# A macaron block with a long convolution: rows turned by VectorE instead of DMA transposes, and work moved between engines and steps

## The chip, the core and the metric

The kernel runs on one core of a Trainium2 chip. Its engines are TensorE (PE: matrix products; PEld is its weight load), VectorE (DVE), ScalarE (ACT), GpSimd (POOL) and SyncE (SP, which here only issues DMAs). Each engine works through its own instructions in order and waits for others by semaphores. The metric is the device time of one execution in microseconds (us).

## The reference

For x of 2 x 1024 rows of 1024 numbers, all float32:

```
x = x + 0.5 * ffn(layernorm(x))
x = x + s4(layernorm(x))
x = x + 0.5 * ffn(layernorm(x))

ffn(x): h = silu(x @ Wg) * (x @ Wu);  return h @ Wd     # 1024 -> 2752 -> 1024
        # weights of 4 bits, with scales and zero points by groups of 128 input rows
s4(x):  causal convolution of every row with a kernel of length 1024
        (made from the state space parameters), plus D[0] * x
```

Both feed-forward layers use the same weights.

## The kernel before

**Jobs.** The 2048 rows are four blocks of 512 (b = 0 to 3). A job is one feed-forward layer (k = 1 or 3) of one block; the eight jobs run in the order `JOBS = [(0,1), (1,1), (0,3), (1,3), (2,1), (3,1), (2,3), (3,3)]`, and the text calls them job 0 to job 7. Each job has an up stage (gate and up products) and a down stage. The convolution (k = 2) of a block runs inside the up stage of the job after its first layer: in jobs 1, 2, 5 and 6.

**Products.** Activations are split into two float16 parts, a high one and a low one (`hi`, `lo`), and each is multiplied by weights held as small whole numbers in bfloat16; so there are two products for each pair of weight chunk and input group. The scale of a group is applied by a rescale: the sum in PSUM is multiplied in place by the ratio of two groups' scales before the next group is added (`scaled`: by ScalarE on line 815, or by VectorE on line 819, as `on_act` says).

The up stage has 64 steps (`STEPS`): eight waves of three, later two, chunks of the inner dimension (`WAVES`), by eight input groups g. A step of three chunks has six units (gate and up of each chunk), 12 products of 512 columns (line 854) and a rescale of each unit; a step of two chunks has four units and eight products, in the last wave one unit more. Even units (gates) are rescaled by ScalarE, odd ones by VectorE, with the exceptions that the diff shows. After a wave's last group, `gated` makes silu(gate) on ScalarE (line 886), the product with the up part on VectorE (`hf`, line 889), and GpSimd makes the two float16 halves of h (`halves`, lines 894 and 895). `watch` puts two more GpSimd operations on a list of chores (lines 905 and 906), which are worked off one at a time.

The down stage has 44 steps, two halves of the output columns by 22 chunks. A step has four PSUM banks, eight products (line 962; the 22nd of each half has four) and four rescales, of which VectorE does two (c = 1 and 3), less those that `relief` names.

**The order of other work.** `hooks` hang work on a step number: `at(up, 36, f)` writes f's instructions ahead of the products of up step 36, and a half (36.5) in the middle of the step. The tile framework then plans the order on each engine by its own costs; `pinned` and `in_order_of_writing` bind instructions of the named engines to the order of writing. Weights are asked for on SP's queue (lines 788 and 795) six steps ahead, in job 0 four.

**Convolution.** For each of the four tiles t of 128 rows: VectorE normalizes and turns the rows in 32x32 blocks (lines 1669, 1673), SP stores them to DRAM (line 1677) and reads them back so that blocks stand in turned order (line 1684). GpSimd then makes sums of columns (lines 1345 to 1347), PE the products with the convolution's Toeplitz blocks in two parts (line 1351), and VectorE adds the results to x (lines 1381 to 1391). Job 1 starts this at step 36 with 3.5 steps between tiles, the others at step 23 with 4. Statistics for the third normalization (`moments_by_tile`, line 191, and `deviations_in_pieces`) follow in the same stage. Job 1's up stage also computes the convolution's kernel (`s4_tables`).

**Input of the next job.** In jobs 1 to 6 the next job's rows are normalized in place (`normalize`, line 274) and turned by `turn_by_dma`: four GpSimd operations make the float16 parts (lines 293 and 295), and two DMA transposes on SP's queue (lines 297 and 298) put them into `pieces`, which the next up stage reads as `xTh` and `xTl`. It hangs at steps 2 to 33 of the down stage. In job 0 the next job's input is turned by PE (`turn_by_pool`). The first job's own input is turned in eight chunks by PE (`first_turn`), ahead of its first steps.

**Results.** A down stage's result y is turned in 32x32 blocks by VectorE (line 1020), stored and read back, and added to x by GpSimd (line 1036).

Of the kernel before, what the change touches and what calls it, by code (L numbers as in the profile page):

```python
# [9 lines left out]
F32 = mybir.dt.float32  # L10
# [35 lines left out]
Q = 32  # L46
# [13 lines left out]
def macaron_s4_kernel(  # L60
# [38 lines left out]
    xpool = ctx.enter_context(tc.tile_pool(name="x", bufs=11))  # L99
    xtpool = ctx.enter_context(tc.tile_pool(name="xT", bufs=1))  # L100
    hpool = ctx.enter_context(tc.tile_pool(name="h", bufs=36))
# [174 lines left out]
    def turn_by_dma(b, t):  # L276

        k = ln[b, t][2]  # L280
        name = f"{b}_{k}_{t}"
        if b not in pieces:
            pieces[b] = [
                xtpool.tile([P, NC, TB], dt, tag=f"xT{w}", name=f"xT{w}_{b}_{k}")
                for w, dt in (("h", F16), ("l", F16))
            ]
        hi_t, lo_t = (a[:, :, bass.ts(t, P)] for a in pieces[b])
        halves = [slice(0, 512), slice(512, HID)]
        n = x[b][t]
        hi = hfpool.tile([P, HID], F16, tag="hf", name=f"hi_{name}")  # L290
        lo = gpool.tile([P, HID], F16, tag="g", name=f"lo_{name}")
        for own in halves:
            nc.gpsimd.tensor_copy(hi[:, own], n[:, own])
            yield
            nc.gpsimd.tensor_tensor(lo[:, own], n[:, own], hi[:, own], ALU.subtract)  # L295
            yield
        nc.sync.dma_start(hi_t, hi, transpose=True)
        nc.sync.dma_start(lo_t, lo, transpose=True)
# [522 lines left out]
    def gate_up(j, b, hooks):  # L821
        hi, lo = pieces[b]
        ps = {}
        for s, (wi, g) in enumerate(STEPS):
# [20 lines left out]
            for i, (k, pos, done) in enumerate(turns):  # L845
# [19 lines left out]
                if g < GK - 1:  # L865
                    on_act = unit % 2 == 0
                    if unit == 2 * fs[0 if n == 3 else 1] + 1:
                        on_act = (j == 0 and n == 3 and g in ((4, 6) if s < 8 else (0, 2, 4, 6)))
                        on_act = on_act or (j < 2 and g % 2 == 0 and (j or n == 2))
                        on_act = on_act or (j in (3, 4) and 24 < s < 33)  # L870
# [13 lines left out]
    def gated(j, f, pg, pu):  # L884
        g = gpool.tile([P, TB], F32, tag="g", name=f"g_{j}_{f}")
        nc.scalar.activation(g, pg, AF.Silu, scale=rat[:, 2 * f, GK - 1 :])  # L886
        hf = hfpool.tile([P, TB], F32, tag="hf", name=f"hf_{j}_{f}")
        last = rat[:, 2 * f + 1, GK - 1 :]
        nc.vector.scalar_tensor_tensor(hf, pu, last, g, ALU.mult, ALU.mult)  # L889
        two = t2(f"h_{j}_{f}").bitcast(F16).rearrange("p (i t) -> p i t", i=2)  # L890
        hi, lo = h[f] = two[:, 0], two[:, 1]

        def halves():
            nc.gpsimd.tensor_copy(hi, hf)  # L894
            nc.gpsimd.tensor_tensor(lo, hf, hi, ALU.subtract)  # L895

        halves()
        watch(hi)

    chores = []  # L900
# [39 lines left out]
    relief = {1: (2, 3, 6, 7, 14, 15, 20), len(JOBS) - 1: (36, 38, 40)}  # L940
# [67 lines left out]
    y_dram = [dpool.tile([TB, 512], F32, tag=f"yz{a}", name=f"yz{a}") for a in range(NH)]  # L1008
    s_dram = [dpool.tile([P, HID], F32, tag=f"sz{i}", name=f"sz{i}") for i in range(2)]
# [621 lines left out]
    def fast():  # L1631
# [5 lines left out]
        for j, (b, k) in enumerate(JOBS):  # L1637
# [7 lines left out]
            if prev:  # L1645
# [9 lines left out]
                if pk == 1:  # L1655
# [23 lines left out]
                    def columns_loaded(t):  # L1679
                        s4x[t] = s = t4(f"st_{pb}_{t}").rearrange("p (c t) -> p c t", c=NC)  # L1680
                        src = s_dram[t % 2].rearrange("(b i) (c a j) -> a i c b j", i=Q, a=NQ, j=Q)
                        for q in range(NQ):
                            dst = s[bass.ts(q, Q)].rearrange("p c (b j) -> p c b j", j=Q)
                            nc.sync.dma_start(dst, src[q])
# [10 lines left out]
                    for t in range(NT):  # L1695
# [6 lines left out]
                        at(up, o + (8 if ahead_of_split else 9), lambda t=t: conv(t))  # L1702
                        at(up, o + 10, lambda t=t: next(parts[t]))
                        at(up, o + 11, lambda t=t: next(parts[t], None))
                    steps = [(up, start_ + gap * t + 13 + i) for t in range(NT) for i in range(2)]
                    steps += [(up, start_ + gap * 3 + 14.5), (up, start_ + gap * 3 + 15)]
                    in_pieces(at, steps, lambda: moments_by_tile(pb, 3, True, LIFT))
                    done = start_ + gap * 3 + 15
                    steps = [(up, 62 + i / 2 if j == 1 else 51.5 + (3 * i // 2) / 2) for i in range(4)]
# [16 lines left out]
            if j == 0:  # L1726
# [25 lines left out]
                first_weights(up, dn, at)  # L1752
            if j == 1:
# [6 lines left out]
            if after:  # L1760
                ab, ak = after
                if ak == 1:
                    at(up, 55 if j == 0 else 6, pinned(lambda: load_x(ab, rows_of(u, ab)), ET.SP))
                    if j == 0:
                        steps = [(up, s) for s in (60.5, 61.5, 62.5)]
                        steps += [(dn, d) for d in (3, 4, 5, 10.5, 11.5, 12)]
                        in_pieces(at, steps, lambda: moments_by_tile(ab, 1, True, LIFT))
                        steps = [(dn, d) for d in (17.5, 18.5, 19, 19.5)]
# [8 lines left out]
                def turning(t):  # L1777
                    if t not in turns:
                        turns[t] = turn_by_dma(ab, t)
                    next(turns[t], None)  # L1780

                for t in range(NT):
                    for half in range(2):
                        d, where = (25 + 4 * t + 2 * half if j == 0 else (2, 6, 14, 20)[t] + half), dn
# [10 lines left out]
                    for d in (1, 3, 5, 7, 9):  # L1795
                        piece = lambda t=t: turning(t)
                        piece = lambda piece=piece: in_order_of_writing(piece, ET.Pool, ET.SP)
                        at(dn, 2 + 7 * t + d + (j == 1 and t == 0), piece)
# [87 lines left out]
    def first_turn(c):  # L1886
# [11 lines left out]
        if c not in (3, 5, 7):  # L1898
# [167 lines left out]
```

## Time and profile before

| | |
|---|---|
| median of 4 runs | 1970.77 us (1970.43 to 1971.83) |
| the profiled execution: its time, its span | 1971.39 us, 1969.3 us |
| granted clock of PE | 0.997 |
| busy: PE, DVE, ACT, POOL | 1927.4, 1627.7, 1403.8, 1044.2 us |
| rescales on ACT, up and down | 1284 x 660 ns, 669 x 662 ns |
| rescales on DVE, up and down | 1124 x 691 ns, 611 x 695 ns |
| 32x32 transposes on DVE (128x256) | 112 x 428 ns for y, 64 x 424 ns for the convolution |
| DMA transposes | 48 |

The span is the time from the first to the last instruction of the program in the profiled execution; what lies around it, here 2.1 us, is in the time of a run as well. Busy time counts an engine as busy while an instruction runs. Product records overlap, since products are pipelined: one of 512 columns has a record of some 379 ns, but in an undisturbed stage one starts every 0.216 us (543 in 117.21 us in job 3's up stage, by the chain).

### The profile page before, as it was taken

To read this page: it belongs to the slowest core of one execution; us is meant where nothing else is said; L and a number is where in the kernel's file an instruction comes from. 1 tells how busy PE (TensorE), PEld (TensorE's weight loads), DVE (VectorE), ACT (ScalarE), POOL (GpSimd) and SP (SyncE) were. 2 spreads that over 40 slices of the span, in tenths; PEclk is the share of its full clock that TensorE was granted. 3 is DMA by queue.
4 is the path that set the end of the run, shared out by engine and by line. 5 is a ranking of instruction groups with operands and counts; after the bars stand their busy time and mean duration, and the time that the engine had idled before them with its cause. 6 is when DMAs were issued, how large, how long until landed. Compare 5 with 4: busy or idle time off the path is not lost.

```text
span 1969.3 us, 28016 instructions
## 1 busy us (share of the span) xinstructions
PE 1927.4 (98%) x9202; PEld 926.8 (47%) x9202; DVE 1627.7 (83%) x2710; ACT 1403.8 (71%) x2205; POOL 1044.2 (53%) x1162
## 2 busy tenths in 40 slices
PE   6999999999999999999999999999999999999998
PEld 3444444464445544444444444456444564444443
DVE  7978878858888788877888778897888978887787
ACT  7888887738775577787777777764777646777776
POOL 5755668748465560656427660563614646345630
PEclk9999999999999999999999999999999999999999
DMA  6557553433635326622473236444264432563225
GB/s 213 194 183 227 175 150 95 119 97 105 202 112 138 94 81 199 211 67 76 128 252 120 69 86 192 134 115 113 77 183 149 124 102 76 153 204 99 73 71 176
DMA packets 320865, 267.34 MB, mean 136 GB/s; under 512 B 141773, under 2 KB 298518, under 8 KB 320710
## 3 DMA queue, kind: packets, MB, share of 16 engines
q1 hardware_dynamic: 319326, 262.87, 45.1%
q10 hardware_dynamic: 1160, 1.90, 0.3%
q8 instruction: 74, 1.21, 0.3%
q0 software_dynamic: 224, 0.69, 0.2%
q14 instruction: 81, 0.66, 0.1%
HBM read 195.58 MB, written 57.02 MB: 128 GB/s over the span
## 4 chain that ended last, share of the span: by engine, by line
PE 83%; DVE 9%; issue 3%; POOL 2%; ACT 1%; DMA 1%; SPq 0%; DVEq 0%; POOLq 0%; ACTq 0%
PE pg L854 50%; PE po L962 29%; DVE pg L819 4%; PE pc L1351 3%; PE pb L1351 1%; DVE hf L889 1%; DVE stats L191 1%; POOL h L895 1%; DVE x L274 0%; DVE xn L1669 0%; POOL h L894 0%; ACT pg L815 0%; DMA w<-wq 0%; ACT g L886 0%; POOL squared L905 0%
## 5 line engine op out<-in xcount | busy, mean ns | idle before, releaser
L815 ACT ACTIVATE pg<-pg,rat 128x512 f32<-128x512 f32 x1284 | 808.4, 660 | 379.5 <-PE pg L854 376.2
L854 PEld LDWEIGHTS <-w 128*128 128x128 bf16 x5504 | 538.1, 98 | 672.3 <-issue 42.7
L819 DVE TENSOR_TENSOR pg<-pg,rat 128x512 f32<-128x512 f32 x1124 | 743.1, 691 | 118.6 <-PE pg L854 114.0
L854 PE MATMUL pg<-xTl,w 128*128 128x512 f16 x2752 | 705.2, 379 | 9.3 <-DVE pg L819 6.8
L854 PE MATMUL pg<-xTh,w 128*128 128x512 f16 x2752 | 701.2, 380 | 3.6 <-ACT pg L815 1.0
L962 PE MATMUL po<-h,wd 128*128 128x512 f16 x2680 | 585.7, 379 | 1.7 <-DVE po L819 1.3
L815 ACT ACTIVATE po<-po,ratd 128x512 f32<-128x512 f32 x669 | 436.7, 662 | 116.3 <-PE po L962 113.8
L819 DVE TENSOR_TENSOR po<-po,ratd 128x512 f32<-128x512 f32 x611 | 422.5, 695 | 83.3 <-PE po L962 81.4
L962 PEld LDWEIGHTS <-wd 128*128 128x128 bf16 x2740 | 267.7, 98 | 325.9 <-issue 9.2
L894 POOL CAST h<-hf 128x512 f16<-128x512 f32 x168 | 106.4, 635 | 353.0 <-DVE hf L889 352.9
L906 POOL TENSOR_TENSOR most<-most,squared 128x512 f32<-128x512 f32 (+1 forms) x176 | 223.9, 1272 | 9.6
L1036 POOL TENSOR_TENSOR x<-x,yr 128x512 f32<-128x512 f32 x52 | 65.7, 1265 | 274.9 <-DMA yr<-yz 274.8
L895 POOL TENSOR_TENSOR h<-hf,h 128x512 f16<-128x512 f32 x168 | 195.5, 1167 | 10.6
L905 POOL TENSOR_TENSOR squared<-h 128x512 f32<-128x512 f16 x168 | 175.6, 1045 | 6.0
L889 DVE SCALAR_TENSOR_TENSOR hf<-pg,rat,g 128x512 f32<-128x512 f32 x168 | 121.0, 746 | 36.7 <-ACT g L886 28.3
L886 ACT ACTIVATE g<-pg,rat 128x512 f32<-128x512 f32 x168 | 110.1, 686 | 21.2 <-PE pg L854 11.7
L191 DVE BATCH_NORM_STATS2 stats<-x 128x6 f32<-128x512 f32 x88 | 59.6, 680 | 0.1
L295 POOL TENSOR_TENSOR lo<-x,hi 128x512 f16<-128x512 f32 x48 | 55.7, 1160 | 2.8
L1381 DVE TENSOR_TENSOR x<-x,pc 128x512 f32<-128x512 f32 x32 | 22.0, 688 | 34.5 <-PE pc L1351 34.5
L1351 PE MATMUL pc<-near,st 128*128 128x256 f32 (+1 forms) x256 | 48.6, 334 | 0.0
L1020 DVE STREAM_TRANSPOSE y<-y 128x256 f32<-128x256 f32 x112 | 47.9, 428 | 0.0
L1351 PEld LDWEIGHTS pc<-near,st 128*128 128x128 f32 x256 | 43.4, 195 | 7.3 <-issue 1.1
(225 smaller groups left out, 830.4 us busy)
## 6 DMA issues: line engine op xcount, KB each, us to landing
w<-wq SPq DMA_DIRECT2D x319, 192.0 KB
wd<-wdq SPq DMA_DIRECT2D x336, 128.0 KB
w<-wq SPq DMA_DIRECT2D x128, 128.0 KB
x<-in_L_attn_u_dram SPq DMA_DIRECT2D x30, 512.0 KB
yz<-y SPq DMA_DIRECT2D x56, 256.0 KB
yr<-yz SPq DMA_DIRECT2D x56, 256.0 KB
w<-wq SPq DMA_DIRECT2D x64, 160.0 KB
sz<-xn SPq DMA_DIRECT2D x16, 512.0 KB
```

Of the source, the lines that this page charges most:

```text
L191: nc.vector.bn_stats(stats[:, t, i, :], x[b][t][:, bass.ts(i, 512)])
L815: nc.scalar.activation(dst, src, AF.Copy, scale=sc)
L819: nc.vector.tensor_tensor(dst, src, sc.to_broadcast(list(dst.shape)), ALU.mult)
L854: product = lambda: nc.tensor.matmul(p, weights, (lo, hi)[k][:, g, :], start=(g == 0 and not done), stop=(g == GK - 1 and done), skip_grou ...
L886: nc.scalar.activation(g, pg, AF.Silu, scale=rat[:, 2 * f, GK - 1 :])
L889: nc.vector.scalar_tensor_tensor(hf, pu, last, g, ALU.mult, ALU.mult)
L894: nc.gpsimd.tensor_copy(hi, hf)
L895: nc.gpsimd.tensor_tensor(lo, hf, hi, ALU.subtract)
L905: chores.append(lambda: nc.gpsimd.tensor_tensor(own, hi, hi, ALU.mult))
L906: chores.append(lambda: nc.gpsimd.tensor_tensor(total, total, own, ALU.add))
L962: nc.tensor.matmul(ps[c], w[:, bass.ts(c, P)], part, start=(f == 0 and k == 0), stop=(f == NF - 1), skip_group_check=True,)
L1351: nc.tensor.matmul(dst, lhsT, rhs, start=start, stop=stop, skip_group_check=True)
```

## The change

- `turn_by_dma` goes. In jobs 1 to 6 the normalized rows are turned in place in 32x32 blocks by VectorE (`turn_blocks`, four operations a tile), stored to DRAM (`store_blocks`) and read back in turned order by four loads (`load_blocks`), and GpSimd splits them into the float16 parts (`split_columns`). Their steps: where the next job has k = 1 (jobs 3 and 4) the turn is in the up stage, elsewhere in the down stage.
- Rescales of one odd unit go to ScalarE in even groups of jobs 2, 5 and 6 too; some more in jobs 3 and 4; `relief` names more down steps in job 1 and new ones in jobs 2, 5 and 6.
- In job 1 the halves of chunks 15 to 18 are put off to steps 50.5, 51.5, 58 and 59; the convolution's sums and products come one step later in job 1, and in each job's last tile; the moments after them half a step later in job 1.
- In job 0 the rows for job 1 are loaded at step 46 instead of 55, their moments are taken in the up stage and the deviations earlier in the down stage. Chunks 4 and 6 of the first input are split by GpSimd instead of ScalarE and VectorE.
- One buffer more for tiles of x, one fewer for h.

```diff
-    xpool = ctx.enter_context(tc.tile_pool(name="x", bufs=11))
+    xpool = ctx.enter_context(tc.tile_pool(name="x", bufs=12))
-    hpool = ctx.enter_context(tc.tile_pool(name="h", bufs=36))
+    hpool = ctx.enter_context(tc.tile_pool(name="h", bufs=35))
...
-    def turn_by_dma(b, t):
...
+    def turn_blocks(b, t, i):
+        own = x[b][t][:, bass.ts(i, 256)]
+        nc.vector.transpose(own, own)
+    def store_blocks(b, t):
+        nc.sync.dma_start(t_dram[t], x[b][t])
+    def load_columns(dst, dram):
+        src = dram.rearrange("(b i) (c a j) -> a i c b j", i=Q, a=NQ, j=Q)
+        for q in range(NQ):
+            part = dst[bass.ts(q, Q)].rearrange("p c (b j) -> p c b j", j=Q)
+            nc.sync.dma_start(part, src[q])
+    def load_blocks(b, t):
+        tile_ = t4(f"turned_{b}_{ln[b, t][2]}_{t}").rearrange("p (c t) -> p c t", c=NC)
+        columns_of[t] = tile_
+        load_columns(tile_, t_dram[t])
+    def split_columns(b, t):
...
+        hi, lo = (a[:, :, bass.ts(t, P)] for a in pieces[b])
+        both = columns_of.pop(t)
+        for half in range(2):
+            own = slice(4 * half, 4 * half + 4)
+            nc.gpsimd.tensor_copy(hi[:, own], both[:, own])
+            yield
+            nc.gpsimd.tensor_tensor(lo[:, own], both[:, own], hi[:, own], ALU.subtract)
+            yield
...
                     if unit == 2 * fs[0 if n == 3 else 1] + 1:
                         on_act = (j == 0 and n == 3 and g in ((4, 6) if s < 8 else (0, 2, 4, 6)))
-                        on_act = on_act or (j < 2 and g % 2 == 0 and (j or n == 2))
-                        on_act = on_act or (j in (3, 4) and 24 < s < 33)
+                        on_act = on_act or (j in (0, 1, 2, 5, 6) and g % 2 == 0 and (j or n == 2))
+                        on_act = on_act or (j in (3, 4) and 24 < s < 40 and (s < 33 or g % 2 == 0))
...
-        halves()
+        if j == 1 and f in WAVES[5] + WAVES[6]:
+            put_off.append(halves)
+        else:
+            halves()
...
-    relief = {1: (2, 3, 6, 7, 14, 15, 20), len(JOBS) - 1: (36, 38, 40)}
+    relief = {1: range(2, 24, 2), len(JOBS) - 1: (36, 38, 40)}
+    for j in (2, 5, 6):
+        relief[j] = range(2, 20, 2)
...
-                        at(up, o + (8 if ahead_of_split else 9), lambda t=t: conv(t))
-                        at(up, o + 10, lambda t=t: next(parts[t]))
-                        at(up, o + 11, lambda t=t: next(parts[t], None))
-                    steps = [(up, start_ + gap * t + 13 + i) for t in range(NT) for i in range(2)]
-                    steps += [(up, start_ + gap * 3 + 14.5), (up, start_ + gap * 3 + 15)]
+                        late = j == 1 or t == NT - 1
+                        at(up, o + (8 if ahead_of_split else 9 + late), lambda t=t: conv(t))
+                        at(up, o + 10 + late, lambda t=t: next(parts[t]))
+                        at(up, o + 11 + late, lambda t=t: next(parts[t], None))
+                    ends = [start_ + gap * t + 13 + (j == 1) / 2 for t in range(NT)]
+                    steps = [(up, e + i) for e in ends for i in range(2)]
+                    steps += [(up, ends[-1] + 1.5), (up, ends[-1] + 2)]
...
+            for d in (50.5, 51.5, 58, 59) if j == 1 else ():
+                at(up, d, lambda: put_off.pop(0)())
...
-                    at(up, 55 if j == 0 else 6, pinned(lambda: load_x(ab, rows_of(u, ab)), ET.SP))
+                    at(up, 46 if j == 0 else 6, pinned(lambda: load_x(ab, rows_of(u, ab)), ET.SP))
                     if j == 0:
-                        steps = [(up, s) for s in (60.5, 61.5, 62.5)]
-                        steps += [(dn, d) for d in (3, 4, 5, 10.5, 11.5, 12)]
+                        steps = [(up, s) for s in (53, 53.5, 54, 54.5, 55, 55.5, 60, 60.5, 61)]
                         in_pieces(at, steps, lambda: moments_by_tile(ab, 1, True, LIFT))
-                        steps = [(dn, d) for d in (17.5, 18.5, 19, 19.5)]
+                        steps = [(dn, d) for d in (3.5, 4, 4.5, 5)]
...
-                        d, where = (25 + 4 * t + 2 * half if j == 0 else (2, 6, 14, 20)[t] + half), dn
+                        d, where = (25 + 4 * t + 2 * half if j == 0 else 2 + 4 * t + half), dn
...
-                    for d in (1, 3, 5, 7, 9):
-                        piece = lambda t=t: turning(t)
-                        piece = lambda piece=piece: in_order_of_writing(piece, ET.Pool, ET.SP)
-                        at(dn, 2 + 7 * t + d + (j == 1 and t == 0), piece)
+                    where, turn, kept, read, part = (
+                        (up, 33 + 2 * t, 35 + 2 * t, 39 + 2 * t, 2 + 3 * t)
+                        if ak == 1
+                        else (dn, 4 + 4 * t, 6 + 4 * t, 9 + 4 * t, 13 + 4 * t)
+                        if j == 1
+                        else (dn, 1 + 4 * t, 3 + 4 * t, 6 + 4 * t, 10 + 4 * t)
+                    )
+                    for i in range(4):
+                        at(where, turn + i / 2, pinned(lambda t=t, i=i: turn_blocks(ab, t, i), ET.DVE))
+                    at(where, kept, pinned(lambda t=t: store_blocks(ab, t), ET.SP))
+                    at(where, read, pinned(lambda t=t: load_blocks(ab, t), ET.SP))
+                    for i in range(4):
+                        at(dn, part + (3 * i // 2) / 2, pinned(lambda t=t: turning(t), ET.Pool))
...
-        if c not in (3, 5, 7):
+        if c < 3:
             nc.scalar.copy(hi, ps)
             nc.vector.tensor_tensor(lo, ps, hi, ALU.subtract)
         else:
```

## The prediction

> **What bounds the kernel now.** I read the page's chain of work that ended last, then busy time by stage, then the chain and the waits of TensorE (PE) inside the stages that stand out.
>
> ```profile
> PE 83%; DVE 9%; issue 3%; POOL 2%; ACT 1%; DMA 1%; SPq 0%; DVEq 0%; POOLq 0%; ACTq 0%
> PE pg L854 50%; PE po L962 29%; DVE pg L819 4%; PE pc L1351 3%; PE pb L1351 1%; DVE hf L889 1%; DVE stats L191 1%; POOL h L895 1%; DVE x L274 0%; DVE xn L1669 0%; POOL h L894 0%; ACT pg L815 0%; DMA w<-wq 0%; ACT g L886 0%; POOL squared L905 0%
> ```
>
> The products are the bound; no edit removes a product, so only time in which PE stands can be won. Busy time by stage (columns: stretch, its length, then busy us and instructions of PE, PEld, DVE, ACT, POOL, then clock, DMA share, GB/s) shows where it stands:
>
> ```profile
> 263.50:453.00 189.50, 182.47 (x905) 96.28 (x904) 147.38 (x277) 128.58 (x209) 127.97 (x170) 0.99 0.40 112
> 527.80:707.20 179.40, 176.54 (x882) 91.58 (x881) 154.89 (x266) 110.62 (x174) 97.72 (x100) 1.00 0.40 115
> 707.20:781.60 74.40, 74.40 (x346) 33.66 (x345) 60.83 (x94) 55.33 (x85) 25.74 (x28) 1.00 0.54 152
> 781.60:930.30 148.70, 148.64 (x689) 67.31 (x688) 122.44 (x198) 114.00 (x181) 87.93 (x87) 1.00 0.39 124
> ```
>
> These are job 1's up stage, job 2's up and down, and job 3's up. Job 3 has no convolution: 688 products in 148.7 us is the floor of an up stage, and 74.4 the floor of a down stage. Jobs 5 and 6 repeat job 2 (179.3, 179.4). What a convolution must cost is read from the last tile of job 1, in the chain in order of time; the same view shows what the first one waits for:
>
> ```profile
> 388.87 1.15 POOL h L895
> 390.02 0.55 POOL h L894
> ...
> 391.83 1.00 POOL sums L1345
> ...
> 435.97 1.75 PE pc L1351 x12
> 437.72 0.22 PE pb L1351 x2
> 437.95 2.65 PE pc L1351 x20
> 440.60 1.56 PE pb L1351 x14
> ```
>
> 6.18 us a tile, 24.7 for four. So job 2's up stage stands 179.4 - 148.7 - 24.7 = 6.0 us, jobs 5 and 6 the same: 18. Job 1's stands 189.5 - 148.7 - 24.7 = 16.1, less at most 4.8 us of products for the tables (L1194 1.8, L1304 2.0, L1277 1.0): 11.3. PE's own waits, first 360 to 455 us, then 615 to 710:
>
> ```profile
> PE pb L1351 <- POOL sums L1345: 5.4, 2, 3.6
> PE pg L854 <- ACT g L886: 0.6, 1, 0.6
> ```
> ```profile
> PE pg L854 <- DVE pg L819: 1.8, 5, 0.7
> PE pb L1351 <- POOL sums L1345: 0.4, 1, 0.4
> PE pg L854 <- ACT pg L815: 0.2, 1, 0.2
> ```
>
> The reader is to see two illnesses: in job 1 the sums stand behind two halves (L894, L895) in POOL's queue, and in jobs 2, 5, 6 rescales come late from a full VectorE (154.9 us in a stage whose products outside the convolution take 148.7). The list holds 2.4 of the 6.0; the rest lies in product records stretched by short waits. All that can be won is about 18 + 11 + a few in job 0.
>
> **The change, part by part.**
>
> *Rescales to ScalarE.* In the up stages of jobs 2, 5, 6 one more unit goes to ACT in the four even groups of each of eight waves: 32 a job, 22 us (0.69 each) off DVE, 21 us (0.66) onto ACT. DVE falls from 155 to 133 of 179, ACT rises from 111 to 132. Waits that DVE ended should mostly go. They come after each convolution (several adds and a rescale pile up) and at the stage's end, when x is normalized (L274). Next in line is ACT in the two-chunk waves: a step is 8 products, 1.73 us, and ACT then has three rescales in even steps, two in odd, and two gates: 18 x 0.66 + 2 x 0.69 = 13.3 of 13.8 us a wave. Queued back to back they pitch shorter, as job 0's timeline shows, five in 3.04:
>
> ```profile
> 156.40 3.04 ACT L815 ACTIVATE pg<-pg,rat 128x512 f32<-128x512 f32 x5 [0.29 <-PE pg L854]
> ```
>
> so 0.61 each, 12.4 of 13.8. Job 1 already runs this split with a convolution; there about 0.26 us is lost when ACT restarts after a tile, and 2.39 us of ACT lie on the chain in its last wave. I leave 2.3 of the 6.0 us: gain 3.7 a job (between 2.0, what the listed DVE and ACT waits hold, and 5.5), 11 for three. In jobs 3 and 4 three more rescales go over; no wait there to win.
>
> *Sums first, later products (job 1, and each last tile).* Four halves are put off to steps 50.5, 51.5, 58, 59, past the sums; products move one step later. A half pair is 0.61 + 1.15 us, two of them 3.5 us: the 3.6 us wait. Gain: the 5.4 us listed, and some of the restarts behind them: 7 (4 to 9). Price: the moments end half a step later, so the deviations lie nearer the stage's end; 0.5 us. The late halves cost nothing themselves: their products come at down steps 15 to 18, over 30 us later; and x rows have 12 buffers for 11, h 35 for 36, with no wait on either pool in the lists, so 0. In jobs 2, 5, 6 the 0.4 us wait is in the 3.7.
>
> *Rows turned by VectorE.* Per tile, 2 DMA transposes (1.25 us of SP's time each) become 4 DVE transposes, one store and four loads; the POOL work is the same four operations. 24 tiles: 96 x 0.43 = 41 us on DVE. Jobs 3 and 4 have them in the up stage, two a step at 33 to 40.5, where DVE (0.82 busy) has room: 0 (to 0.4 each). In the down stages of jobs 2, 5, 6, 4 x 0.43 = 1.7 us per four steps meets two rescales given to ACT, 1.4: even, but the first pair falls on steps 1 and 1.5, before any relief and while DVE still clears the last chunks: +0.3 each (0 to 0.7). In job 1's down stage x is normalized in the same steps, every two steps then hold 3 x 0.69 + 1.7 = 3.8 of 3.46 us by mean durations, though queued ones overlap by 0.1 each: +0.3 (0 to 1.5). These 1.2 us are paid; the transfer is not, as long as the prefetch covers it. It reads as the convolution's does, and the page by stretch shows one such read-back and one pair of DMA transposes:
>
> ```profile
> 605.00:610.00 5.00, 5.00 (x25) 2.25 (x23) 4.63 (x9) 3.62 (x7) 2.08 (x3) 1.00 0.89 236
> 726.00:731.00 5.00, 5.00 (x25) 2.27 (x24) 4.02 (x7) 3.88 (x6) 4.76 (x7) 1.00 0.95 179
> ```
>
> Both fill the engines, PE does not stand. The packet records say why they are equal: 4096 packets of 128 bytes at 12.9 ns are 3.31 us of sixteen engines, 2048 packets of 256 bytes at 27.8 ns are 3.56; the store adds 1.27. [...] The rows above are of this very read-back, whose runs are 32 elements since VectorE has already turned the blocks, so I take them.
>
> *Job 0.* Two of the first turns go from DVE (2 x 0.69 off) to POOL (2 x 1.77 on), at 31 and 38 us, where the chain runs through POOL (L685 four times, 3.13, then L410 to L412). Cost 0.5, between -1 (DVE was late there by 0.5 at 43.9) and +2.5 (all of one turn ahead of the scales, and more). Moments move from six places in the down stage to the up stage: 5 statistics of 0.68 leave a down stage that stands about 3 us, and come into steps 53 to 55.5, where DVE idles 1.9 us before the gates. -0.5 (-2 to +2). The rows of x for it, 2 MB, are loaded at step 46 instead of 55, ahead of weight loads on SP, some 10 us at that stage's 210 GB/s; it was as long at 55, and no wait for weights shows there: 0 (to 1). Job 0 together 0.
>
> **Sum.** -11 - 7 + 0.5 + 0.9 + 0.3 + 0 = -16.3, say -16.5. The profiled execution had 1969.3 us of span and 2.1 around it, 1971.4, which is 0.6 over the median of 1970.8. So the span goes to about 1952.8, the median to 1954.3.
>
> **Rivals.**
>
> *Only the POOL waits go (0.17).* ACT takes DVE's place in the narrow waves: 13.3 of 13.8 us leaves nothing for restarts, and job 1's last wave already ends on ACT. Then jobs 2, 5, 6 gain about 1 each: -3 - 7 + 1.7 + 0.5 = -8, 1963. Against it, the 0.61 pitch.
>
> *Nothing net (0.08).* The order on the engines is a planner's; with other lengths it can put the sums behind the halves again, or the late products against the next wave's banks. Then no step does what it says: 1967 to 1974.
>
> *SP's queue, slower (0.10).* Place: the 24 read-backs. SP works in order; a load that waits for its store to land holds the weight loads behind it. In 600 to 700 us SP already stood this long for one store:
>
> ```profile
> SPq L1714 <- DVE x L1391: 7.0, 1, 7.0
> ```
>
> Weights are asked for six steps ahead, 6 x 1.73 = 10.4 us in a down stage, and take about 3 us to come: it decides from about 7.4 us of standing. To eat the gain it needs 9 us at 16 tiles: 16 x 1.6 = 26 us, so 1980. Against it: the convolution's store and load, two steps apart, cause no wait for weights (1.3 us in all of the kernel's listed waits on w), and here three or four steps lie between.
>
> The other 0.65 is the forecast, by itself 1946 to 1961.
>
> **Numbers.** A measurement here can tell about 0.2%, 4 us, from no change. Faster: the forecast 0.65 and the first rival 0.15 of its 0.17: 0.80. Same: 0.09, from the second rival and the end of the first. Slower: 0.11, SP's queue and a bad start of job 0. The range runs from 1945 (nearly all 29 us but the price of the turns) to 1967, where the slower rival and some of the second are left out.
>
> **What would show it.** Up stages of jobs 2, 5, 6 at 175 to 176 us, DVE near 133 busy in them and ACT near 132; job 1's up near 183 with no wait on sums over 1 us; down stages under 75; no DMA_TRANSPOSE; 96 more of DVE's transposes; some 133 rescales fewer on L819 (96 and 6 up, 4 and 27 down). Wrong if PE waits for w, if up stages of jobs 2, 5, 6 keep over 178 us with ACT as releaser, or if job 0 grows by over 3 us.

## The result, and the profile after

The change does not make the kernel faster: 1972.4 us (median of 40 runs) against 1969.6 us (median of 60 runs of the kernel before beside them), ratio 1.0013 with a 95% interval of 1.0009 to 1.0018, so it is 2.8 us slower. The forecast was 1954.3. The profiled execution has a span of 1969.9 us, before 1969.3. The chain of work that ended last, by engine and by line:

```profile
PE 85%; DVE 7%; POOL 4%; issue 3%; ACT 1%; DMA 0%; ACTq 0%; POOLq 0%; DVEq 0%
PE pg L871 51%; PE po L984 29%; PE pc L1374 3%; DVE pg L836 2%; PE pb L1374 1%; POOL h L912 1%; DVE hf L906 1%; DVE po L836 1%; DVE x L274 1%; POOL most L926 1%; POOL h L911 1%; POOL squared L925 0%; DVE xn L1692 0%; ACT g L903 0%; ACT pg L832 0%
```

DVE's rescales of the up stages on the chain (pg L836, before pg L819) fell from 4% to 2%, as meant; POOL rose from 2% to 4%: its halves (L911, L912) and its chores (L925, L926). Busy time by stage of the kernel after, with the columns of the prediction's table. The rows are job 0 from its third step, job 1 up and down, job 2 up and down, job 3 up:

```profile
26.80:264.00 237.20, 232.35 (x1100) 107.27 (x1099) 196.66 (x325) 195.67 (x320) 153.71 (x199) 1.00 0.61 194
264.00:454.50 190.50, 183.44 (x905) 97.70 (x904) 148.21 (x276) 128.96 (x209) 128.15 (x170) 0.98 0.40 112
454.50:530.90 76.40, 75.12 (x345) 33.63 (x344) 64.38 (x110) 60.02 (x95) 55.90 (x54) 1.00 0.63 176
530.90:709.00 178.10, 175.97 (x881) 91.55 (x880) 136.24 (x234) 126.62 (x206) 97.82 (x100) 1.00 0.41 116
709.00:783.70 74.70, 74.65 (x346) 33.69 (x345) 59.25 (x101) 59.20 (x94) 26.03 (x28) 1.00 0.66 180
783.70:932.80 149.10, 148.87 (x689) 67.26 (x688) 124.94 (x211) 115.34 (x184) 87.97 (x87) 1.00 0.51 152
```

Two stages of before that the prediction did not show, the same part of job 0 and job 1's down stage:

```profile
28.50:263.50 235.00, 231.22 (x1101) 107.42 (x1100) 196.67 (x325) 196.28 (x320) 149.02 (x195) 1.00 0.61 194
453.00:527.80 74.80, 74.56 (x345) 33.64 (x344) 62.52 (x97) 57.90 (x91) 56.01 (x54) 1.00 0.53 152
```

Stage by stage, measured to 0.01 us from a stage's first product to the next stage's first:

| stage | before | after | difference |
|---|---|---|---|
| start, to job 0's third step | 28.48 | 26.77 | -1.71 |
| rest of job 0 | 234.98 | 237.27 | +2.29 |
| job 1 up | 189.55 | 190.48 | +0.93 |
| job 1 down | 74.80 | 76.41 | +1.61 |
| jobs 2, 5, 6 up, each | 179.38 | 178.07 | 3 x -1.31 |
| jobs 2, 5, 6 down, each | 74.40 | 74.65 | 3 x +0.25 |
| jobs 3, 4 up, each | 148.72 | 149.17 | 2 x +0.45 |
| jobs 3, 4 down, job 7 up | | | 0 |
| job 7 down, to the end | 85.02 | 84.80 | -0.22 |

The start is chance: in the profile of before the granted clock is 0.50 from 24.58 to 27.99 us, so that job 0's second step takes 4.29 us and not 2.60. The same half clock appears in three experiments that have the changed job 0, and in no other profile. Job 7's down stage, which no edit touches, takes 84.5 to 86.7 us in the twelve profiles. Without these two rows the sum is +2.6 us, and the medians differ by 2.8. PE's waits in the changed kernel, in three stretches: 360 to 456 us, job 2's up stage, job 1's down stage:

```profile
PE pb L1374 <- POOL sums L1368: 6.1, 2, 3.1
```
```profile
PE pg L871 <- DVE pg L836: 1.0, 2, 0.8
PE pb L1374 <- POOL sums L1368: 0.5, 1, 0.5
PE pg L871 <- ACT pg L832: 0.2, 1, 0.2
```
```profile
PE po L984 <- DVE po L836: 1.2, 3, 0.6
```

The wait for the sums that was to go is still there, 6.1 us where it was 5.4. The waits that VectorE ends in job 2 are nearly halved. Job 1's down stage has three, 1.2 us in all, where it had one of 0.2.

### The profile page after: what moved, and what is told of

Read it like the earlier page. It is cut to its first block, busy times and chain, and to the rows that moved or that the text cites. A ratio compares the mean times of both kernels' runs of the same rounds, so it can differ in the third digit from the quotient of the medians.

```text
span 1969.9 us, 28221 instructions
## 1 busy us (share of the span) xinstructions
PE 1928.7 (98%) x9202; PEld 928.0 (47%) x9202; DVE 1573.9 (80%) x2671; ACT 1467.9 (75%) x2338; POOL 1050.1 (53%) x1166
## 4 chain that ended last, share of the span: by engine, by line
PE 85%; DVE 7%; POOL 4%; issue 3%; ACT 1%; DMA 0%; ACTq 0%; POOLq 0%; DVEq 0%
PE pg L871 51%; PE po L984 29%; PE pc L1374 3%; DVE pg L836 2%; PE pb L1374 1%; POOL h L912 1%; DVE hf L906 1%; DVE po L836 1%; DVE x L274 1%; POOL most L926 1%; POOL h L911 1%; POOL squared L925 0%; DVE xn L1692 0%; ACT g L903 0%; ACT pg L832 0%
## 5 line engine op out<-in xcount | busy, mean ns | idle before, releaser
L832 ACT ACTIVATE pg<-pg,rat 128x512 f32<-128x512 f32 x1386 | 860.5, 661 | 333.7 <-PE pg L871 329.1
L836 DVE TENSOR_TENSOR pg<-pg,rat 128x512 f32<-128x512 f32 x1022 | 677.3, 692 | 153.9 <-PE pg L871 149.2
L832 ACT ACTIVATE po<-po,ratd 128x512 f32<-128x512 f32 x700 | 449.6, 662 | 105.0 <-PE po L984 102.4
L836 DVE TENSOR_TENSOR po<-po,ratd 128x512 f32<-128x512 f32 x580 | 399.8, 694 | 90.0 <-PE po L984 88.4
L911 POOL CAST h<-hf 128x512 f16<-128x512 f32 x168 | 106.4, 635 | 349.7 <-DVE hf L906 347.2
L926 POOL TENSOR_TENSOR most<-most,squared 128x512 f32<-128x512 f32 (+1 forms) x176 | 224.3, 1274 | 10.0
L912 POOL TENSOR_TENSOR h<-hf,h 128x512 f16<-128x512 f32 x168 | 195.5, 1167 | 10.8
L925 POOL TENSOR_TENSOR squared<-h 128x512 f32<-128x512 f16 x168 | 176.1, 1048 | 6.5
L314 POOL TENSOR_TENSOR xTl<-turned,xTh 128x512 f16<-128x512 f32 x48 | 55.4, 1155 | 3.4
L312 POOL CAST xTh<-turned 128x512 f16<-128x512 f32 x48 | 29.3, 610 | 42.1 <-DMA turned<-tz 39.9
L1368 POOL TENSOR_TENSOR sums<-st 128x384 f32<-128x384 f32 x16 | 16.1, 1008 | 58.6 <-PE pb L1374 48.0
```

What stands on the lines that cost most here:

```text
L832: nc.scalar.activation(dst, src, AF.Copy, scale=sc)
L836: nc.vector.tensor_tensor(dst, src, sc.to_broadcast(list(dst.shape)), ALU.mult)
L925: chores.append(lambda: nc.gpsimd.tensor_tensor(own, hi, hi, ALU.mult))
L926: chores.append(lambda: nc.gpsimd.tensor_tensor(total, total, own, ALU.add))
```

## The experiments

Each kernel is the changed kernel with the edit shown, unless it says otherwise; ratios are to the kernel before, run on the same chip.

**Are the late halves late?** In the changed kernel POOL's queue around the first and the third tile of job 1's convolution reads so (start, us, instruction):

```profile
391.05 0.61 POOL L911 CAST h<-hf 128x512 f16<-128x512 f32 x1
391.74 1.15 POOL L912 TENSOR_TENSOR h<-hf,h 128x512 f16<-128x512 f32 x1
392.85 1.17 POOL L1368 TENSOR_TENSOR sums<-st 128x384 f32<-128x384 f32 x1
...
419.28 0.61 POOL L911 CAST h<-hf 128x512 f16<-128x512 f32 x1 [13.46 <-DVE hf L906]
...
422.87 0.99 POOL L1368 TENSOR_TENSOR sums<-st 128x384 f32<-128x384 f32 x1
```

The halves still stand ahead of the sums. At 419.28 POOL had idled 13.46 us for a product of VectorE, with sums queued behind it whose data had been read back by 407.2 us. The first experiment binds the halves to the place where they are written:

```diff
-                at(up, d, lambda: put_off.pop(0)())
+                at(up, d, pinned(lambda: put_off.pop(0)(), ET.Pool))
```

> The changed kernel with one line more: the halves that are put off in job 1 are bound to GpSimd's order of writing, so behind the sums. Theory A (the planner kept the halves ahead of the sums, and PE waits for that): job 1's up stage falls from 190.5 to about 182 us, PE's wait on the sums from 6.1 us to under 1, the kernel by 8 to 9 us against the changed one. Rival (the sums wait for the read-back or for their tile, whatever stands before them): job 1's up stage stays within 1 us of 190.5.

Measured: 1962.25 us, ratio 0.9967 (0.9954 to 0.9979). Its POOL queue at the same two tiles, and job 1's up stage:

```profile
389.09 0.99 POOL L1368 TENSOR_TENSOR sums<-st 128x384 f32<-128x384 f32 x1
...
421.88 1.00 POOL L1368 TENSOR_TENSOR sums<-st 128x384 f32<-128x384 f32 x1 [5.82 <-PE pb L1374]
```
```profile
264.00:444.80 180.80, 179.97 (x906) 94.76 (x905) 147.48 (x276) 128.95 (x209) 128.09 (x170) 1.00 0.42 118
```

No wait for sums is left, and the stage fell from 190.48 to 180.78. This is 9.7 us for waits that add up to 6.1. The granted clock has the rest: 0.98 over the stage in the changed kernel, 1.00 here. Around the second wait of the changed kernel, in stretches of 3.41 us:

```profile
419.83:423.24 3.41, 0.98 (x8) 0.77 (x6) 0.83 (x2) 0.00 (x0) 3.25 (x5) 1.00 0.12 40
423.24:426.65 3.41, 2.74 (x9) 2.38 (x10) 1.73 (x4) 0.00 (x0) 3.33 (x5) 0.50 0.00 0
426.65:430.07 3.42, 3.42 (x18) 3.42 (x17) 0.21 (x1) 0.00 (x0) 0.64 (x1) 0.50 0.00 0
430.07:433.48 3.41, 3.41 (x23) 2.27 (x23) 2.33 (x4) 1.01 (x2) 1.83 (x3) 1.00 0.00 0
```

PE stood 3.10 us, to 423.91; the clock was 0.50 for 6.83 us, in which products took about twice as long: eight of the convolution's (`pc<-near`) took 1.30 us at 418.90, from the first one's start to the next product's, and eight took 2.56 at 424.50. The step that holds this wait (56) is 6.3 us longer than the same step here: 3.1 of waiting and 3.2 of half clock. The other 3.3 us are the first wait, which no low clock followed.

**What do the turns cost?** DMA transposes put back (`turn_by_dma` with its steps), the rescales that went to ScalarE for the turns' sake back on VectorE, and the normalise in job 1's down stage at its old steps.

> The changed kernel with DMA transposes again, and the down stage's relief and the steps of normalizing as before. Theory (the turn on VectorE costs what the stages show): job 1's down stage 76.4 to 74.8 us, jobs 2, 5, 6 down 74.65 to 74.4, jobs 3 and 4 up 149.2 to 148.7; the kernel 3.3 us less than the changed one. Rival (the stage differences come from other edits): down stages within 0.2 us of the changed kernel's.

Measured: 1970.61 us, ratio 1.0004 (0.9994 to 1.0013). Job 1's down stage is as before the change, to 0.1 us:

```profile
454.90:529.70 74.80, 74.70 (x346) 33.66 (x345) 62.79 (x98) 57.95 (x91) 55.96 (x54) 1.00 0.55 152
```

76.41 went to 74.74 there, 149.17 to 148.72 in jobs 3 and 4, 74.65 to 74.60 in jobs 2, 5, 6: the turn, with the steps that go with it, costs 1.67 + 0.90 + 0.15 = 2.7 us. By the medians the whole kernel fell by 1.8; the difference to 2.7 lies within the interval.

**What are the rescales on ScalarE worth?** Undone in the up stages of jobs 2, 5, 6:

```diff
-                        on_act = on_act or (j in (0, 1, 2, 5, 6) and g % 2 == 0 and (j or n == 2))
+                        on_act = on_act or (j in (0, 1) and g % 2 == 0 and (j or n == 2))
```

> The changed kernel with the odd units of jobs 2, 5 and 6 on VectorE again in the up stage. Theory (the relief alone is what shortened these stages, 1.3 us each): up stages of jobs 2, 5, 6 go from 178.07 back to 179.4, the kernel 4 us slower than the changed one. Rival (the later products did it): they stay at 178 to 178.4.

Measured: 1979.11 us, ratio 1.0048 (1.0031 to 1.0065). Job 2's up stage, and PE's waits in it:

```profile
532.00:712.40 180.40, 176.58 (x882) 91.46 (x881) 154.78 (x266) 110.59 (x174) 97.88 (x100) 1.00 0.40 114
```
```profile
PE pg L871 <- DVE pg L836: 1.8, 5, 0.7
PE pb L1374 <- POOL sums L1368: 1.3, 1, 1.3
```

180.40 against 178.07: the relief is worth 2.33 us a job. 180.40 is also 1.02 above the kernel before, where the wait for the sums was 0.4: that is the price of the last tile's products one step later, which the relief had to pay first.

**Is it POOL's work that slows VectorE?** In the changed kernel the normalise of x (L274) in job 2's up stage takes two lengths. VectorE, then POOL in the same stretch:

```profile
687.52 0.54 DVE L274 TENSOR_SCALAR x<-x,mv,r 128x512 f32<-128x512 f32 x1
...
691.79 1.46 DVE L274 TENSOR_SCALAR x<-x,mv,r 128x512 f32<-128x512 f32 x1
...
693.77 1.46 DVE L274 TENSOR_SCALAR x<-x,mv,r 128x512 f32<-128x512 f32 x1
```
```profile
691.12 0.61 POOL L911 CAST h<-hf 128x512 f16<-128x512 f32 x1 [5.25 <-DVE hf L906]
691.81 1.16 POOL L912 TENSOR_TENSOR h<-hf,h 128x512 f16<-128x512 f32 x1
692.90 0.81 POOL L911 CAST h<-hf 128x512 f16<-128x512 f32 x1
693.79 1.16 POOL L912 TENSOR_TENSOR h<-hf,h 128x512 f16<-128x512 f32 x1
```

The fourth experiment leaves POOL's chores of jobs 2, 5, 6 out:

```diff
-        watch(hi)
+        if j not in (2, 5, 6):
+            watch(hi)
```

> The changed kernel without the chores of jobs 2, 5 and 6 (the squares of h and their sum for the range test are left out there, so less is tested). Theory B (the normalizing operations of VectorE run 0.54 us when GpSimd is idle and up to 1.5 when it works, and that makes the waits that the relief left): these operations fall towards 0.54 where only chores ran beside them, up stages of jobs 2, 5, 6 from 178.1 to about 176.5. Rival (VectorE's queue is simply too long after convolution and gates): within 0.3 us of 178.1.

Measured: 1970.76 us, ratio 1.0006 (0.9996 to 1.0015). The up stages went from 178.07 to 177.31, not to 176.5: a stand of 0.72 us in step 36 is gone, with as many instructions on VectorE (234 in both); that of 1.22 in step 57 stays, which lies beside halves and not beside chores, and the two normalises there still take 1.45 and 1.46.

**The last tile's sums.** The first experiment's edit, and in jobs 2, 5, 6 the sums of the last tile ahead of the halves, as those of tiles 0 and 2 are:

```diff
-                        if j != 1 and t % 2 == 0:
+                        if j != 1 and (t % 2 == 0 or t == NT - 1):
...
-                                splits_after[j, start_ + gap * t + 8 + s] = sums
+                                splits_after[j, start_ + gap * t + 8 + 2 * (t % 2) + s] = sums
```

> The changed kernel with job 1's late halves bound to their place in POOL's queue (as in the first experiment, which took 9.7 us off job 1's up stage), and in jobs 2, 5 and 6 the sums of the last tile of the convolution ahead of the halves of the wave's first gates, as those of tiles 0 and 2 already are. If the fault of the sums is the same there (one halves pair that waits for a product of ScalarE and VectorE stands in front of finished data), the last tile's step goes from 7.16 us of convolution to the 6.2 of the other tiles, an up stage from 178.07 to about 177.1, and the kernel to about 1959.8 (9.7 and 2.9 under the changed kernel's 1972.4). If what is lost at the last tile is its later products and VectorE's backlog, jobs 2, 5, 6 stay at 178.1 and the time is 1962.5.

Measured: 1960.53 us, ratio 0.9953 (0.9938 to 0.9968). The last tile's step went from 7.16 to 6.38 us of convolution, an up stage to 177.30, 0.77 a job of the 0.96 expected.

**Normalise where POOL is idle.** The sums-first kernel with

```diff
-                            d, where = (54 if ak == 3 else 25) + 2 * t + half, up
+                            d, where = 25 + 2 * t + half, up
+                            if ak == 3:
+                                d = (53.5, 59.5, 60.5, 61.5)[t] + half / 2
```

> The same as the sums-first kernel, and in jobs 2, 5 and 6 six of the eight half tiles of x are normalized 1 to 5 steps later (59.5 to 62 in place of 56 to 61), where POOL stands idle, not beside POOL's halves and chores of chunks 17 and 18. If VectorE's 128x512 SBUF normalise is stretched by POOL at work beside it (0.54 us alone, up to 1.46 beside it), all eight come down to about 0.54 to 0.6, the stall of 1.21 us in step 57 goes to about 0.3, and an up stage falls by 0.9 us: about 2.7 us in all. If POOL has nothing to do with it and it is only VectorE's number of instructions, the normalise keeps its lengths, the stall moves to steps 60 to 63 and the stage stays within 0.3 us.

Measured: 1958.53 us, ratio 0.9940 (0.9925 to 0.9955). Seven of the eight normalises in job 2 now take 0.53 to 0.55, the eighth, which a chore of POOL still meets, 1.27; the stand in step 57 is gone, one of 0.79 in step 60 came, and an up stage is 176.59: 0.71 a job, not 0.9.

**Job 0 as before**: five first turns on VectorE's side, rows of x loaded at step 55, moments in the down stage.

```diff
-                    at(up, 46 if j == 0 else 6, pinned(lambda: load_x(ab, rows_of(u, ab)), ET.SP))
+                    at(up, 55 if j == 0 else 6, pinned(lambda: load_x(ab, rows_of(u, ab)), ET.SP))
...
-                        steps = [(up, s) for s in (53, 53.5, 54, 54.5, 55, 55.5, 60, 60.5, 61)]
+                        steps = [(up, s) for s in (60.5, 61.5, 62.5)]
+                        steps += [(dn, d) for d in (3, 4, 5, 10.5, 11.5, 12)]
...
-                        steps = [(dn, d) for d in (3.5, 4, 4.5, 5)]
+                        steps = [(dn, d) for d in (17.5, 18.5, 19, 19.5)]
...
-        if c < 3:
+        if c not in (3, 5, 7):
```

> The changed kernel with job 0 as in the kernel before (five first turns on VectorE's side and not three, rows of x loaded at step 55, moments in the down stage). If the change in job 0 costs by the two turns on POOL (1.9 us of standing in step 6, before 0.6) and the moments before the gates, the first pass over step 6 falls to about 0.6, the end of job 0 counted from its first product comes about 0.6 us sooner (up 162.9 to 163.4, down 82.5), and the kernel is some 0.6 us faster, hardly to be told in the median. If the 0.6 us are chance of the start, the end of job 0 stays at 264 within the 0.6 us by which the runs differ.

Measured: 1971.09 us, ratio 1.0001 (0.9992 to 1.0010). Counted from job 0's third step, to be free of the start, its rest takes 235.03 us (before 234.98, after 237.27, the other kernels with the changed job 0 236.5 to 237.7): 2.2 us, not 0.6. My expectation had counted from the first product, where the chance of the start lies. Steps 2 to 10 of the up stage hold 2.0 of it, 1.3 of them step 6. The chain of the changed kernel shows what goes ahead of that step, as start, us, what:

```profile
38.64 0.56 POOL xTh L1936
39.20 0.31 POOL safe L427
...
39.94 1.16 POOL xTl L1937
...
41.18 0.47 POOL safe L428
```

A first turn's two pieces stand between the steps of the scales that PE's rescales wait for; undone, step 6's stand falls from 1.91 to 0.64. The moments before the gates add 0.3 in steps 54 to 60. The kernel as a whole gained less than 2.2, since job 1's up stage came out at 191.80: there the first wait for sums, 3.01 us, came with half clock as well, where 3.00 us in the changed kernel had not.

**All of it**: sums first and bound, normalise spread, DMA transposes, job 0 as before; the rescales of the up stages stay on ScalarE.

> What the experiments point to: the rescales on ScalarE kept; sums first, and bound; normalise spread; DMA transposes in place of VectorE's turns; job 0 as before. If the costs add: 1972.4 - 9.7 (job 1's sums) - 2.9 (last tiles) - 2.7 (normalise) - 2.7 (turns) - 0.6 (job 0) = 1953.8, ratio to the kernel before 0.992, with no stage over its floor by more than 3 us but job 0 and the last down stage. If the spread normalise or the last tiles bring nothing, 1956.5 to 1959.

Measured: 1953.36 us, ratio 0.9916 (0.9903 to 0.9930). The 1953.8 was a sum in part of effects as expected; with those measured it is 1972.4 - 9.7 - 2.3 - 2.1 - 2.7 - 2.2 = 1953.4, so the single effects add up. Job 1 up and down, job 2 up:

```profile
261.50:442.40 180.90, 179.94 (x906) 94.77 (x905) 147.76 (x276) 128.94 (x209) 127.62 (x170) 1.00 0.42 117
442.40:517.10 74.70, 74.61 (x345) 33.65 (x344) 62.72 (x98) 57.85 (x91) 55.94 (x54) 1.00 0.55 152
517.10:693.70 176.60, 175.26 (x882) 91.51 (x881) 134.71 (x234) 126.94 (x206) 97.38 (x100) 1.00 0.41 117
```

**POOL's chores moved, none left out.** The all-mended kernel with

```diff
-                if 0 < s % GK < GK - 1:
+                if 0 < s % GK < GK - 1 and not (j in (2, 5, 6) and 33 <= s < 37):
...
-                                d = (53.5, 59.5, 60.5, 61.5)[t] + half / 2
+                                d = (53.5, 60, 61, 62)[t] + half / 2
```

> The all-mended kernel with two things moved in jobs 2, 5, 6 and nothing added or left out: POOL's chores (L949, L950 there) have no places behind steps 33 to 36 and so run later, not beside VectorE's normalise of the convolution's columns, and the normalise of x's tiles 1 to 3 comes half a step later still. If VectorE's SBUF normalise is slow because POOL works beside it, the two xn normalises near 615 us fall from 1.40 and 0.88 to about 0.54 each, the stall of 0.71 us in step 36 goes, and that in step 60 (0.78) falls to 0.4 or less: 1.0 us a job, 3 in all, 1950.4. If the stall of step 36 is VectorE's queue of adds and rescales behind the tile, it stays at 0.7 and the time within 0.5 of the all-mended kernel's 1953.4.

Measured: 1958.67 us, ratio 0.9937 (0.9923 to 0.9951): slower than the all-mended kernel by 5, where 3 less were expected. Near step 36 one chore fewer runs; of the two normalises of xn, the convolution's copy of x, one fell from 0.88 to 0.53, the other kept its 1.40, and the stand from 0.71 to 0.37. But the chores that moved run later, and now meet x's normalise. VectorE, then POOL:

```profile
672.22 1.57 DVE L274 TENSOR_SCALAR x<-x,mv,r 128x512 f32<-128x512 f32 x1
...
686.05 2.39 DVE L274 TENSOR_SCALAR x<-x,mv,r 128x512 f32<-128x512 f32 x2
```
```profile
672.24 1.26 POOL L950 TENSOR_TENSOR most<-most,squared 128x512 f32<-128x512 f32 x1
...
685.71 1.04 POOL L949 TENSOR_TENSOR squared<-h 128x512 f32<-128x512 f16 x1
686.83 1.33 POOL L950 TENSOR_TENSOR most<-most,squared 128x512 f32<-128x512 f32 x1
```

The normalise at 672.22 is at the place that it had before, where it took 0.55; only the chore beside it is new. Two new stands of 1.27 us came, in steps 54 and 61, that of 0.78 in step 60 went, and the up stage went from 176.56 to 177.99. So the theory behind the expectation held in both directions and its number failed: I had not followed where the chores would go.

**The turn in job 1's down stage.** The changed kernel without the chores of jobs 1, 3 and 4 (`if j not in (1, 3, 4)` ahead of `watch(hi)`), one profile.

> The changed kernel without POOL's chores of jobs 1, 3 and 4 (squares of h and their maximum, so the range test sees less). For the price of the turn in job 1's down stage, 76.41 us against 74.80 before. If the turn's load alone overfills VectorE there (3.8 us of work to 3.46 us of products, as forecast, the transposes being what is new), the stage stays at 76.2 or more and its stalls in steps 4, 8 and 12 (0.40, 0.76, 0.50) stay. If it is the normalise of x in the same steps, stretched by POOL (second of each pair 1.09, 1.46, 1.19 us against 0.53), those come down to 0.54 and the stage to about 75.0. In the up stages of jobs 3 and 4 the 0.45 us of the turn would likewise go or stay.

Measured: 1972.43 us, one run. The normalise pair of x's tile 1, in the changed kernel and here:

```profile
466.72 0.53 DVE L274 TENSOR_SCALAR x<-x,mv,r 128x512 f32<-128x512 f32 x1
...
468.31 1.46 DVE L274 TENSOR_SCALAR x<-x,mv,r 128x512 f32<-128x512 f32 x1
```
```profile
468.52 0.53 DVE L274 TENSOR_SCALAR x<-x,mv,r 128x512 f32<-128x512 f32 x1
...
470.11 0.54 DVE L274 TENSOR_SCALAR x<-x,mv,r 128x512 f32<-128x512 f32 x1
```

The stage fell from 76.41 to 75.29: by this one profile 1.1 of the turn's 1.67 us are POOL's chores meeting the normalise, which leaves VectorE no room for the transposes. Of the rest, 0.4 lie in step 4, where POOL's last halves (to 463.6 us in this run) meet the first pair, and one normalise still takes 1.10 us. The 0.45 us in jobs 3 and 4 stay; the last tile's transposes stand between gates and rescales at the end of a wave there (step 41, 0.32), which no run took apart.

## Why the prediction was wrong

What it took as its second rival, 0.08, is what happened in job 1: the planner's order put the sums behind the halves again. That alone does not make the miss, as the terms show:

| term | forecast | measured |
|---|---|---|
| rescales to ScalarE, three up stages | -11 | 3 x -2.33 = -7.0, and +0.6 in the down stages behind |
| later products of the last tile | in the -11 | 3 x +1.02 = +3.1 |
| sums first in job 1, moments later | -6.5 | +0.9 |
| the turn | +1.2 | +2.7 |
| job 0 | 0 | +2.3 |
| sum | -16.3 | +2.6 |

Of the 18.9 us between the two sums, 7.4 are the sums first, 7.7 the rescales with the later products, 1.5 the turn and 2.3 job 0. With the halves bound the kernel took 1962.25: inside the forecast's range, and still 8 us above 1954.3.

**Sums first is the step that failed.** I read "put off to steps 50.5, 51.5, 58, 59, past the sums" in the code as the order in POOL's queue. It is only the order of writing, which the planner may change, and it did: a plain `at` where the neighbours use `pinned`. The forecast needed that order read from the program, not from the steps. The mechanism was right, and its gain was put too low: bound, the sums bring 189.55 - 180.78 = 8.8 us against the kernel before, where I had put 7, between 4 and 9. About 1.7 of the 8.8 are a term that the prediction left out: 3.41 us of half clock behind the wait of 3.56.

**The rescales** did what was said: DVE in job 2's up stage 154.9 to 136.2 us, 133 rescales fewer (1735 to 1602). The wait for ScalarE that the list shows is 0.2 us as before, but the list leaves out waits under 0.15 us, and there the first rival is partly right: in the two-chunk waves, odd steps 43, 45 and 51 take 1.92 us and not 1.73, and the product that is late in each waits for a rescale of ScalarE. The even steps that VectorE held up (1.99 in step 44, 1.84 in step 50) are at 1.73 in their place. From step 41 to 55, the last tile's step aside, the relief gained under 0.1 us; its 2.33 lie elsewhere, 0.7 of them in the last tile's step. An up stage fell by 1.31 net, near the rival's "about 1", and stays at 178.07, over the 178 that the prediction named as a sign against itself. (The rival's sum of -8 has 0.5 more than its terms give: the price of 1.7 holds the moments already.) Beside this the term was mis-sized by what "a full VectorE" took in: 2.0 us a job of the 6.0 (0.71, 1.11 and 0.16 in steps 36, 57 and 58; 0.72, 1.22 and 0.16 after) lie where POOL holds up a normalise, and stayed though VectorE had 32 rescales less; and the last tile's later products, which I put under a 0.4 us wait that was to go, took 1.0. The +0.2 in each down stage is not the turn's: undoing the turn took away 0.05, and without the relief the stage is 74.45.

**The turn** was forecast at 1.2, between 0 and 4.4 by its own bounds (0.7 three times, 1.5, and 0.4 twice), and took 2.7: in job 1 1.67 where I had 0.3, of which one profile puts 1.1 down to POOL's chores, and 0.9 in jobs 3 and 4, put at 0. The 3.8 us of work in two steps that the prediction counted there, against 3.46 of products, are those of the transposes; the two steps between hold the normalises, at tile 1 3 x 0.69 + 0.53 + 1.46 = 4.1, which it did not count. The transfer is hidden, as forecast: in job 2's down stage the DMA share rose from 0.54 to 0.66 and PE waits for no weights, so the third rival, SP's queue, is out. It also allowed about 3 us for a weight load, where one in the kernel before is asked for at 930.51 us and has its last packet at 932.20, 1.69 us later. The rows of the convolution's read-back were the right ones to take: there a tile's 4096 packets of 128 bytes hold sixteen engines for 3.31 us, and those of the four tiles in job 2's down stage of the changed kernel for 3.32 each.

**Job 0** was bounded for the two turns between -1 and +2.5, and the value taken, 0.5, was read from no row. With both turns in the chain that the prediction itself named, +2.0 is near its upper end. The moments gave 0.3 the other way: what left the down stage brought 0.07 there, since steps 4 and 14 got shorter by 0.34 together and step 17 longer by 0.28.

## What to carry to other kernels

Where a planner orders the queues, an edit of the place where something is written is worth nothing until the order of the engine's queue is read: one `pinned` was the difference between +0.9 and -8.8 us. A long instruction is not always a slow engine: split one line's durations by what the neighbour engine does at the time, before the wait behind it is put down to load, and when the neighbour's work is moved, look where it lands. And waits on the matmul engine are to be priced with the clock that comes with them, not by their length alone: in the changed kernel one of 3.10 us came with 3.2 us of half clock, one of 3.00 us with none.

## What the runs showed of the hardware

**VectorE's normalise beside a busy POOL.** In the changed kernel the 128x512 normalise of x takes 0.53 to 0.54 us whenever POOL is idle (24 of them) and 0.91 on average, up to 1.47, where POOL works for more than half of it (29, of which five keep 0.53 to 0.55). Rescales (0.69) and transposes (0.425) are the same beside a busy POOL as beside an idle one. In the slow ones looked at, the time added stayed under the length of the POOL instruction met: 0.92 us at 691.79, beside one of 1.16, and, with the chores moved, 1.03 at 672.22 beside one of 1.26. The rows do not show what lengthens the normalise, nor which of two instructions that start 0.02 us apart came first. In the other direction, a chore of POOL that began at 466.89, inside the normalise at 466.72, took 1.25 us, where the one at 464.42 took 1.04. The longer normalise was in the kernel before, too (0.54 us beside an idle POOL, 22 of them, and 0.86 on average, up to 1.36, beside a busy one, 31), behind waits that I put down to VectorE's load.

**The clock after a wait.** Stands of PE for sums came with a clock of 0.50 at 3.56 us (the kernel before) and 3.10 (the changed kernel), and not at 1.81 (the kernel before). At 3.00 and 3.01 us it went both ways; the first product after the wait shows which, in the changed kernel and in the one with job 0 undone:

```profile
394.08 0.49 PE L1374 MATMUL pb<-near,sums 128*128 128x128 f32 x2 [3.00 <-POOL sums L1368]
```
```profile
391.89 0.80 PE L1374 MATMUL pb<-near,sums 128*128 128x128 f32 x2 [3.01 <-POOL sums L1368]
```

In the profiles of before and after, any two changes of the clock lie a whole multiple of 3.413 us apart, to 0.01 us (in the kernel before 368.64 us, 108 of them, lie between the starts of its first two half clocks). In windows of this length cut at these points, half clock began five times in the two profiles (two of them behind the last products of the program), each time after a window at full clock in which PE was busy for 0.37 of the time or less; the other 1133 windows at full clock were busy for 0.50 or more, and full clock went on after every one. So in these profiles it is not the length of a stand but its place in the windows that goes with the clock. The 3.00 us of the changed kernel fell into two windows, the 3.01 us of the other mostly into one:

```profile
389.11:392.52 3.41, 1.97 (x13) 1.65 (x12) 1.76 (x3) 0.86 (x2) 3.18 (x5) 1.00 0.78 251
392.52:395.93 3.41, 1.85 (x12) 1.75 (x13) 1.89 (x4) 0.00 (x0) 3.33 (x5) 1.00 0.02 4
```
```profile
387.99:391.41 3.42, 0.89 (x8) 0.67 (x6) 2.07 (x2) 0.00 (x0) 3.34 (x4) 1.00 0.42 132
391.41:394.82 3.41, 2.93 (x9) 2.57 (x10) 2.10 (x3) 0.00 (x0) 2.79 (x4) 0.50 0.00 0
```

The 6.83 us after the stand of 3.10 are two windows: PE was busy for 0.80 of the first, which was followed by a second at half clock, and for all of that one, after which the clock was 1.00. The half clock in job 0's second step of the kernel before came after a window with stands of 1.00 and 1.27 us (busy 0.33). What lies between 0.37 and 0.50 did not occur in these two profiles, and no experiment set out to make it.
